# Mamba scan: softplus as one table function on ScalarE, and a seventh group per step with du by DMA

## The chip, the cores and the metric

The kernel runs on one core of a Trainium2 chip. The metric is the device time of one execution in microseconds. The core has five engines with an instruction queue each: TensorE (PE), VectorE (DVE), ScalarE (ACT), GpSimd (POOL) and SyncE (SP, which here only issues DMAs), and 16 DMA engines beside them.

## The reference

The reference is a chain of four blocks on an image of shape 4 x 96 x 64 x 64: Mamba, an SSD block, Mamba again (other weights), and a ConvNeXt block. The change touches the two Mamba blocks alone. A Mamba block has two layers, each over a sequence of 4096 tokens:

```python
dbl = xc @ xproj_w
dt = dbl[..., :DTRANK]
Bm = dbl[..., DTRANK:DTRANK + DSTATE]
Cm = dbl[..., DTRANK + DSTATE:]
delta = jax.nn.softplus(dt @ dt_w + dt_b)
A = -jnp.exp(A_log)
dA = jnp.exp(delta[..., None] * A)
dBx = delta[..., None] * Bm[:, :, None, :] * xc[..., None]
...
hstates = jax.lax.associative_scan(comb, (dA, dBx), axis=1)[1]
y = jnp.einsum('blds,bls->bld', hstates, Cm) + Dp * xc
y = y * jax.nn.silu(z)
return y @ out_w
```

Here 192 channels have 16 states each, so that a layer has 3072 independent first-order recurrences. `xc` is the convolved input after SiLU, `z` the gate.

## The kernel before

`program` (L1799) runs `mamba_fusion`, `ssd`, `mamba_fusion`, `convnext` one after the other. A Mamba block is cut into **steps**: one image (4), one layer (2) and one chunk of 1024 tokens (4) make a step, so there are 32 steps in a block and 64 in the kernel.

A step has two parts. The **front** (`mamba_front`, L158) makes what the scan needs: layer norm, the in-projection joined with the convolution (L207, copied from PSUM at L213, SiLU over all three tiles at L215), the gate z (L223), `dbl` (L238 to L242), then softplus for three tiles of 128 x 512 (`begin`, L254: a matmul `pt` and `softplus`, L333). `softplus` works on ScalarE with the one table set that holds exp and ln: Abs, Exp, Ln, and two Identity passes that recover the rounding lost in 1 + u. The rest of it is one VectorE operation per tile (`rest`, L266) and two GpSimd operations (`lost` L270, `size` L274). `sized` (L277) makes du = delta * x on GpSimd. delta and du go to DRAM (`store`, L282, as dd and dg), and B and C come back from DRAM copied over the partitions (L293, tile bc).

The **scan** (`Scan`, L346) cuts a step into 24 **groups** of 128 x 1024 (8 channels of each half of the tokens by 16 states): three tiles j, four quarters q, two halves p, in this order. I call a group's number in its step, 0 to 23, its place. For each group:

- `load` (L363) fetches delta rows from DRAM, copied over the 16 states (da, two DMAs of 256 KB);
- `spread` (L375): in an ordinary group TensorE spreads du into PSUM (bs, L384). In a **DMA group** du comes by two more DMAs from dg, ScalarE writes the exponential of da to bs in PSUM instead, and `product` (L390) multiplies du by B on GpSimd (L392);
- `decay` (L398): the exponential of da in place, on ScalarE, in an ordinary group;
- `scan` (L402) on VectorE: in an ordinary group first the product of bs and B (L407), then the recurrence along the tokens (L412);
- `after` (L415): GpSimd multiplies the states by C (hc, L419), ScalarE copies the last column (carry, L422);
- `sums` (L424), `close` (L445) and `project` (L452): TensorE adds over the states into py, VectorE multiplies by the gate (y, L450), TensorE projects.

Before the change a step has six DMA groups, at places 1, 5, 9, 13, 17 and 21. Which comes when is written out by hand in `run` (L472): iteration n calls the stages for groups at fixed distances (load 5 ahead, spread 1 ahead, decay and product 2 ahead, scan at n, after 1 behind), then advances the front of the next step by a number of its `yield` segments that the table PACE (L324) gives, then py's sums and the projections. What is recorded so is chained in order on each engine (L537 to L542): each engine runs its instructions strictly in this order. The front of the next step begins 8 groups before the step ahead of it starts (LEAD), so PACE's entry k falls in place (k + 16) mod 24. The front of the very first step of a block runs alone, ahead of the scan.

ScalarE's table sets are kept by `Tables` (L96): `exp_ln` uses the standing set; `other` loads another set first and, with `back`, the standing set again behind it.

Buffers that matter: tile tag da (da and du loads) has 8, bs in PSUM 2, the front's PSUM tag mm 2, hs 4, hc 5.

## Time and profile before

| What | Value |
|---|---|
| median of 3 runs | 8700.51 us (8700.26 to 8705.55) |
| the profiled execution's own time | 8698.77 us |
| its span | 8697.1 us |
| mean granted TensorE clock | 0.93 |
| busy over the span: PE, DVE, ACT, POOL | 84%, 88%, 66%, 79% |
| first Mamba scan, 76 to 2900 us: DVE, POOL, ACT busy | 2614, 2588, 1819 us of 2824 |
| SSD, 2900 to 5000 us: DVE, POOL, ACT busy | 1698, 1403, 1613 us of 2100 |
| second Mamba scan, 5400 to 8100 us: DVE, POOL, ACT busy | 2557, 2556, 1760 us of 2700 |
| DMA share in the same three stretches | 0.83, 0.33, 0.85 |

The profile is of one execution. Busy time of an engine is the time in which one of its instructions runs; the DMA share is the mean busy share of the 16 DMA engines. A group is all instructions of one line, engine, operation and shape, with its count, its busy time and the mean length of one; what follows is the engine's idle time just before them and who ended it. In a timeline each row has start, length, engine, line, operation and tiles, and in brackets the idle time ahead of it with the instruction that ended it. An instruction's length is longer than its distance to the next one where both overlap.

### The profile page before, as it was taken

To read this page: it belongs to the slowest core of one execution; us is meant where nothing else is said; L and a number is where in the kernel's file an instruction comes from. 1 tells how busy PE (TensorE), PEld (TensorE's weight loads), DVE (VectorE), ACT (ScalarE), POOL (GpSimd) and SP (SyncE) were. 2 spreads that over 40 slices of the span, in tenths; PEclk is the share of its full clock that TensorE was granted. 3 is DMA by queue.
4 is the path that set the end of the run, shared out by engine and by line. 5 is a ranking of instruction groups with operands and counts; after the bars stand their busy time and mean duration, and the time that the engine had idled before them with its cause. 6 is when DMAs were issued, how large, how long until landed. Compare 5 with 4: busy or idle time off the path is not lost. (4 is left out here: it accounts for less than half of the span.)

```text
span 8697.1 us, 112655 instructions
## 1 busy us (share of the span) xinstructions
PE 7340.2 (84%) x34200; PEld 3243.1 (37%) x34200; DVE 7621.2 (88%) x8769; ACT 5778.7 (66%) x10726; POOL 6909.6 (79%) x4653
## 2 busy tenths in 40 slices
PE   7888888888887898998988887888888888887588
PEld 1222222222221687887887884122222222221122
DVE  6999999999998687887888886999999999999786
ACT  5666667666664777777777776666666666666255
POOL 6999999999998565665766765999999999999321
PEclk8999999999998899999999998999999999999799
DMA  6888888888886323333333234888888888888553
GB/s 176 221 223 235 219 222 229 221 225 227 226 220 178 105 88 98 101 90 96 103 94 105 86 90 118 214 220 232 224 219 229 224 226 225 229 222 222 127 126 80
DMA packets 800712, 1524.98 MB, mean 175 GB/s; under 512 B 115565, under 2 KB 121481, under 8 KB 797034
## 3 DMA queue, kind: packets, MB, share of 16 engines
q1 hardware_dynamic: 797034, 1512.67, 65.8%
q8 instruction: 273, 4.47, 0.2%
q10 hardware_dynamic: 3072, 5.11, 0.2%
q14 instruction: 333, 2.73, 0.1%
HBM read 1222.55 MB, written 148.50 MB: 158 GB/s over the span
## 5 line engine op out<-in xcount | busy, mean ns | idle before, releaser
L419 POOL TENSOR_TENSOR hc<-hs,bc 128x1024 f32<-128x1024 f32 x1536 | 3602.1, 2360 | 299.9 <-DVE hs L412 291.6
L412 DVE TENSOR_TENSOR_SCAN hs<-da,carry,bs 128x1024 f32<-128x1024 f32 x864 | 2027.4, 2347 | 129.2 <-issue 51.7
L384 PE MATMUL bs<-du,seldu 64*128 64x512 f32 x4608 | 1481.1, 709 | 684.0 <-DVE hs L412 667.5
L407 DVE TENSOR_TENSOR bs<-bs,bc 128x1024 f32<-128x1024 f32 x1152 | 1396.9, 1213 | 20.3 <-PE bs L384 19.6
L110 ACT ACTIVATE da<-da,w_a 128x1024 f32<-128x1024 f32 x1152 | 1301.7, 1139 | 1.5
L384 PEld LDWEIGHTS bs<-du,seldu 64*128 64x128 f32 x4608 | 409.7, 202 | 1765.8 <-issue 894.9
L433 PE MATMUL py<-hc,selsum 128*32 128x512 f32 x6144 | 876.2, 633 | 92.3 <-DVE y L450 63.3
L392 POOL TENSOR_TENSOR du<-du,bc 128x1024 f32<-128x1024 f32 x384 | 907.5, 2363 | 12.3 <-DMA du<-dg 12.3
L110 ACT ACTIVATE bs<-da,w_a 128x1024 f32<-128x1024 f32 x384 | 428.5, 1116 | 583.9 <-DVE hs L412 459.5
L207 PE MATMUL pu<-h,w_conv 96*64 96x512 f32 (+1 forms) x3072 | 808.3, 645 | 7.8 <-ACT h L196 7.2
L1334 POOL TENSOR_TENSOR y<-y,xs 128x192 f32<-128x192 f32 x496 | 292.9, 591 | 654.5 <-DVE y L1327 615.6
L412 DVE TENSOR_TENSOR_SCAN hs<-bs,carry,du 128x1024 f32<-128x1024 f32 x288 | 670.7, 2329 | 58.6 <-DMA dd<-delta 34.3
L1155 DVE SCALAR_TENSOR_TENSOR bc<-front,taps,bc 128x342 f32<-128x342 f32 (+1 forms) x1152 | 656.9, 571 | 64.1 <-ACT bc L1147 35.9
L412 DVE TENSOR_TENSOR_SCAN hs<-da,bs 128x1024 f32<-128x1024 f32 x288 | 658.4, 2286 | 42.0 <-issue 15.1
L110 ACT ACTIVATE seg<-seg,ndac 128x128 f32<-128x128 f32 x1536 | 502.8, 390 | 246.8 <-POOL seg L1234 244.7
L1123 PE MATMUL front<-sconv,pk 128*128 128x192 f32 x3072 | 606.6, 335 | 0.4
L1265 POOL TENSOR_TENSOR xs<-x,coef 128x576 f32<-128x576 f32 x512 | 589.5, 1151 | 16.7 <-DVE y L1343 14.7
L1234 POOL TENSOR_TENSOR seg<-dr,mask 128x384 f32<-128x384 f32 x512 | 511.5, 999 | 8.3 <-DMA dr<-rows 8.3
L1123 PEld LDWEIGHTS front<-sconv,pk 128*128 128x128 f32 x3072 | 517.0, 196 | 2.7 <-ACT dtrow L900 1.3
L1680 DVE SCALAR_TENSOR_TENSOR acc<-strips,kern,acc 128x512 f32<-128x512 f32 x504 | 426.1, 847 | 53.2 <-ACT acc L1670 36.7
L463 PE MATMUL po<-y,w_out 64*96 64x512 f32 x768 | 446.2, 679 | 0.0
L422 ACT COPY carry<-hs 128x1 f32<-128x1 f32 x1152 | 203.4, 180 | 363.5 <-DVE hs L412 362.8
(231 smaller groups left out, 13504.6 us busy)
## 6 DMA issues: line engine op xcount, KB each, us to landing
da<-dd SPq DMA_DIRECT2D x3072, 256.0 KB
du<-dg SPq DMA_DIRECT2D x768, 256.0 KB
dr<-rows SPq DMA_DIRECT2D x256, 384.0 KB
bc<-rows SPq DMA_DIRECT2D x256, 256.0 KB
dd<-delta SPq DMA_DIRECT2D x192, 256.0 KB
dg<-du SPq DMA_DIRECT2D x192, 256.0 KB
pk<-xn SPq DMA_DIRECT2D x128, 384.0 KB
pk<-xn SPq DMA_DIRECT2D x128, 256.0 KB
```

Of the source, the lines that this page charges most:

```text
L110: self.last = self.scalar.activation(out, in_, func, **kw)
L207: nc.tensor.matmul(pu[HALFP * i : HALFP * (i + 1)], lhsT=wt["conv"][:kk, tap, D0[j] : D0[j] + HALFP], rhs=h[:kk, ds(i * T + tap, T)], star ...
L384: nc.tensor.matmul(g["bs"][:, i], lhsT=self.sel["du"][rows, g["half"], g["q"]], rhs=g["made"]["du"][rows, g["j"]], start=True, stop=True,)
L392: self.tc.nc.gpsimd.tensor_tensor(g["du"], g["du"], self.b_or_c(g, 0), ALU.mult)
L407: nc.vector.tensor_tensor(dbx, dbx, self.b_or_c(g, 0), ALU.mult)
L412: nc.vector.tensor_tensor_scan(out, da, dbx, init, ALU.mult, ALU.add)
L419: nc.gpsimd.tensor_tensor(g["hc"], hs, self.b_or_c(g, 1), ALU.mult)
L433: nc.tensor.matmul(py[ds(HALFP * i + QUART * x["half"], QUART)], lhsT=self.sel["sum"][:, q], rhs=x["hc"][:, i], start=(q == 0), stop=(q == ...
L1123: nc.tensor.matmul(p, lhsT=held["pk"][:, i, ds(c * Q, Q)], rhs=self.conv[:, i], start=(i == 0), stop=(i == 2),)
L1155: nc.vector.scalar_tensor_tensor(out, shifts[tap], self.taps[:, q, tap : tap + 1], out, ALU.mult, ALU.add)
L1234: self.nc.gpsimd.tensor_tensor(seg, g["pair"]["dr"][:, ds(g["c"] % 2 * NH, NH)], self.mask[:, g["r"]].to_broadcast([P, NH, Q]), ALU.add,)
L1265: self.nc.gpsimd.tensor_tensor(xs, x.to_broadcast([P, 3, NH, HD]), coef.to_broadcast([P, 3, NH, HD]), ALU.mult)
```

## The change

Softplus becomes one table function (Softplus) on ScalarE, for three tiles in a row between two loads of table sets. The VectorE operation and two of the three GpSimd operations per tile go, and with them tile v. Place 7 becomes a DMA group in each step, so there are seven: 1, 5, 7, 9, 13, 17 and 21. Tag da gets 9 buffers. PACE is written anew: with it SiLU of x moves from place 5 to place 7, all three softplus tiles fall in place 13 (before: 11, 12 and 14), bc's loads in 14 (before: 13). Tag ua has 3 buffers in all its uses, and the layer norm's rs has two of its own. An unused helper `softplus_tail` goes too.

```diff
-    kept = []
-    def begin(j):
-        pt = bank("pt")
...
-        kept.append(softplus(nc, k.act, work, pt))
-    def rest(j):
-        delta, t, u, v, x = kept[j]
-        nc.vector.scalar_tensor_tensor(delta, x, 0.0, t, ALU.max, ALU.add)
-    def lost(j):
-        u, v = kept[j][2:4]
-        nc.gpsimd.tensor_tensor(v, u, v, ALU.subtract)
-    def size(j):
-        delta, v = kept[j][0], kept[j][3]
-        nc.gpsimd.tensor_tensor(delta, delta, v, ALU.add)
+    def sizes():
+        deltas = []
+        for j in range(3):
+            pt = bank("pt")
+            for i in range(2):
+                half = ds(HALFP * i, HALFP)
+                nc.tensor.matmul(
+                    pt[half], lhsT=wt["dt"][half, D0[j] : D0[j] + HALFP], rhs=dbl[half], start=True,
+                    stop=True,
+                )
+            delta = work.tile([P, T], F32, name="delta", bufs=3)
+            k.act.other(delta, pt, AF.Softplus, back=(j == 2))
+            deltas.append(delta)
+        return deltas
     def sized(j):
-        nc.gpsimd.tensor_tensor(du[:, j], kept[j][0], made["x"][:, j], ALU.mult)
+        nc.gpsimd.tensor_tensor(du[:, j], deltas[j], x[:, j], ALU.mult)
...
-    begin(0)
+    deltas = sizes()
     yield
-    begin(1)
-    yield
-    rest(0)
-    lost(0)
     for i in range(2):
         for q in range(2):
...
+    sized(0)
     yield
-    size(0)
-    rest(1)
-    begin(2)
-    yield
-    sized(0)
-    lost(1)
-    rest(2)
+    store(0)
     gate(2)
     yield
-    store(0)
-    size(1)
-    yield
     sized(1)
-    lost(2)
     yield
     store(1)
-    size(2)
     yield
     sized(2)
...
 PACE = {
-    0: 2, 1: 1, 2: 1, 3: 1, 4: 1, 6: 1, 7: 2, 8: 2, 9: 1, 10: 1, 11: 2, 12: 2, 13: 1, 15: 1, 16: 2,
-    17: 1, 18: 1, 19: 1, 20: 1, 21: 1, 22: 1, 23: 1, 24: 1, 25: 1, 26: 1, 27: 1, 28: 1, 29: 1,
+    0: 2, 1: 1, 2: 1, 3: 1, 4: 1, 6: 1, 7: 1, 8: 2, 9: 1, 10: 1, 11: 1, 12: 2, 13: 1, 14: 1, 15: 1,
+    16: 1, 17: 2, 18: 1, 19: 1, 21: 1, 22: 1, 23: 1, 25: 1, 26: 1, 27: 1, 28: 1, 29: 1,
 }
...
-            g[name] = self.state.tile([P, GS, T], F32, tag="da", name=name, bufs=8)
+            g[name] = self.state.tile([P, GS, T], F32, tag="da", name=name, bufs=9)
...
-                last=(q == NQU - 1 and p == 1), dma=(q % 2 == 0 and p == 1),
+                last=(q == NQU - 1 and p == 1), dma=(p == 1 and (q % 2 == 0 or (j, q) == (0, 3))),
```

## The prediction

> **What bounds the kernel now.** I took the busy line by stage first, since the change touches only the two Mamba scans; then the groups of one such stage, then the engines' timelines over one step. The busy line is for 450 to 2450 us (columns: stretch, length, PE, PEld, DVE, ACT, POOL, granted clock, DMA share, GB/s):

> ```profile
> 450.00:2450.00 2000.00, 1707.96 (x6655) 417.39 (x6654) 1900.77 (x1191) 1339.67 (x2067) 1907.01 (x923) 0.94 0.86 225
> ```

> VectorE and GpSimd are both 95% busy; ScalarE has a third free. One step of 24 groups takes 84.67 us (the same y close, L450, stands at 1200.85 and 1285.52 in VectorE's timeline), and there are 64 steps (dd is stored 192 times, 3 a step). The groups of 600 to 2400 us, with count, busy time and mean:

> ```profile
> L419 POOL TENSOR_TENSOR hc<-hs,bc 128x1024 f32<-128x1024 f32 x512 | 1200.0, 2358 | 84.5 <-DVE hs L412 81.6 <-PE py L433 1.3 <-DMA da<-dd 1.2
> ...
> L407 DVE TENSOR_TENSOR bs<-bs,bc 128x1024 f32<-128x1024 f32 x383 | 464.5, 1213 | 2.6 <-PE bs L384 2.5
> ...
> L392 POOL TENSOR_TENSOR du<-du,bc 128x1024 f32<-128x1024 f32 x127 | 299.9, 2362 | 0.0
> ...
> L274 POOL TENSOR_TENSOR delta<-delta,v 128x512 f32<-128x512 f32 x63 | 80.4, 1276 | 0.0
> ...
> L266 DVE SCALAR_TENSOR_TENSOR delta<-pt,lg 128x512 f32<-128x512 f32 x63 | 41.9, 665 | 0.0
> ```

> GpSimd waits for VectorE's scans (hc), so VectorE leads most of the time. Its timeline shows where it doesn't, once a step, at the sixth DMA group (place 21):

> ```profile
> 1259.28 2.35 DVE L412 TENSOR_TENSOR_SCAN hs<-da,carry,bs 128x1024 f32<-128x1024 f32 x1
> 1262.92 2.35 DVE L412 TENSOR_TENSOR_SCAN hs<-bs,carry,du 128x1024 f32<-128x1024 f32 x1 [1.29 <-POOL du L392]
> ```
> ```profile
> 1256.98 1.28 POOL L274 TENSOR_TENSOR delta<-delta,v 128x512 f32<-128x512 f32 x1
> 1258.23 2.35 POOL L419 TENSOR_TENSOR hc<-hs,bc 128x1024 f32<-128x1024 f32 x1
> 1260.54 2.35 POOL L392 TENSOR_TENSOR du<-du,bc 128x1024 f32<-128x1024 f32 x1
> ```

> B's product ends at 1262.89, the scan starts at 1262.92: GpSimd was late, having the nine short softplus operations between its products. The stalls of this kind sum to 27.7 us in 1800, or 1.3 a step. (Most are put down to a DMA of dd, but there too the product ends last: at 1008.64 for a scan at 1008.68.) From one start to the next, as instructions overlap, a scan takes 2.26 us, a DMA group's 2.24, L407 1.36 with its hand-over, L266 0.58.

> Last, ScalarE's timeline around SiLU of x, which now falls in place 5:

> ```profile
> 1205.22 0.19 ACT L422 COPY carry<-hs 128x1 f32<-128x1 f32 x1 [0.93 <-DVE hs L412]
> 1207.52 0.58 ACT L213 COPY x<-pu 128x512 f32<-128x512 f32 x1 [2.11 <-PE pu L207]
> 1208.12 1.28 ACT L115 ACT_TABLE_LOAD   x1
> 1209.41 1.48 ACT L115 ACTIVATE x<-x 128x1536 f32<-128x1536 f32 x1
> 1210.91 1.28 ACT L122 ACT_TABLE_LOAD   x1
> 1212.21 1.15 ACT L110 ACTIVATE da<-da,w_a 128x1024 f32<-128x1024 f32 x1
> ```

> Scan 5 began at 1205.10; ScalarE is free for exponentials again 7.11 us later. The next one that VectorE needs straight from PSUM (bs of place 9) is three groups off, so this costs nothing today.

> [...] the trace has 0.58 to 0.69 for its ScalarE operations of 512. [...]

> **The change, part by part.** Durations are the profiled execution's (8698.77 us, span 8697.1; 1.7 below the median).

> *Softplus on VectorE and GpSimd.* Three L266 go: 3 x 0.58 = 1.74 us a step from the engine that bounds. Six short GpSimd operations go, 6 x 1.245 = 7.5 us, and with them the stall at place 21, 1.3 us: behind product 21 only one `sized` is left in that place, and the hc ahead of it is no longer late. What is late next is VectorE itself.

> *Seventh DMA group, place 7.* VectorE loses one L407 and gains 0.02 on the scan: 1.36 + 0.02 = 1.38 us. GpSimd gains one product, 2.33; its sum is 31 x 2.33 + 3 x 1.245 = 76.0 us a step, under VectorE's. Places 5, 7 and 9 are crowded: from the end of scan 4 GpSimd does hc 4, product 7, hc 5, hc 6, product 9, five times 2.33 = 11.7 us, and VectorE reaches scan 9 at 2.24 + 3.62 + 2.24 + 3.62 = 11.7: just in time, counted as nothing. PE loses two matmuls, nothing. SP issues two more DMAs, 1.2 us of a queue that waits 516 of these 1800 us for buffers; the ninth buffer lets it load as far ahead as before (30 tiles in 8, 31 in 9). DMA: a step's 0.86 x 84.67 = 72.8 us is some 72.5 transfers of 256 KB, 1.0 us each; two more make 74.8. In 600 to 2400 us I counted packets off against issues: a da load lands 2.2 to 7.4 us after issue, and its load is called five groups ahead, so nothing here.

> Gain: 1.74 + 1.30 + 1.38 = 4.42 us in a step with a front beside it.

> *Given back, place 9.* The new pace puts SiLU of x in place 7, and the compiled order of ScalarE has carry 6, the x copy, load, SiLU, load, and directly after it the exponential of bs 9. Zero is the start of scan 7: ScalarE is free at 7.11 (the chain above, the same PE work ahead of it), bs 9 is there at 7.11 + 1.12 + 0.05 = 8.28. VectorE has scan 7 (now a DMA group, no L407), L407 8 and scan 8: 2.24 + 1.36 + 2.26 = 5.86, and scan 9 has nothing else to do. **Stall 2.4 us.** Queued behind it is VectorE's whole row; GpSimd waits with it.

> *Given back, place 15.* The three softplus matmuls now stand together in place 13 (a DMA group, 2.24 us long), ahead of the projection and of bs 15. PE from the start of scan 13: hand-over 0.23, bs 14 1.06, three pt of 1.04, projection 1.03, bs 15 1.06: 6.5 us. VectorE wants bs 15 at 5.86. **Stall 0.7 us** with its hand-over. Softplus itself isn't in the trace: I take 0.6 us; below 0.58 no operation of that shape lies, above I bound it by SiLU's 1.48, three times as long. At 0.6 it ends the third at 5.1 and the exponential of place 16 at 7.5, needed at 9.5: hidden. ScalarE: load 1.28, three at 0.6, load 1.28 in place of 3 x 3.1 us. The third pt reuses the first one's PSUM bank (there are two): at 0.6 softplus 0 frees it at 3.0 and PE gets there at 3.4, at 1.48 PE waits and the stall grows by 0.6.

> *Other moves.* bc's four loads start one place later (14), needed by place 1 of the next step: nothing. First dd and dg are stored one place earlier, nothing. The two fronts ahead of the scans (at 40 to 76 us and near 5360) run uncovered: ScalarE spends 48.92 to 62.34 from the first Abs to the last load, some 8.5 with the table function, and first loads go out at 61.1 after GpSimd's chain; I take 5 us each, between 0 and 7.

> Sum for each scan of 32 steps: 32 x 1.38 + 31 x (1.74 + 1.30) - 31 x (2.4 + 0.7) = 44.2 + 94.2 - 96.1 = 42.3 (31, as the last step has no front beside it). Two scans and two starts: 84.6 + 10 = 95 us. **8700.5 - 95 = 8605**, a step of 83.3 us. Its own range: the stalls of 2.4 and 0.7 may be 0.4 off each way (62 x 0.8 = 50) or the softplus at 1.48 (37): 8555 to 8660.

> **Rivals.** *The two stalls don't come* (PE or ScalarE gets ahead in a way that I don't see): 44.2 + 94.2 doubled is 277, plus 10: 8414. For it: VectorE never waits long for ScalarE now. Against: the order on ScalarE is fixed, and its chain is measured.

> *DMA becomes the bound.* The place is the loads of da and du in every step, the price set by the busy share s that 16 engines can hold: a step is 74.8 / s. The share that I forecast is 74.8 / 83.3 = 0.90. From s under 0.90 it eats the gain, at 74.8 / 84.67 = 0.883 nothing is left, at today's 0.86 a step is 87.0, so 64 x 2.3 = 147 us slower: **8850**. For it: 0.86 is already the highest of any stage, and over bc's loads and the stores (1235 to 1255) it stands at 0.9 to 1.06. Against: that very stretch shows that 0.9 and more can be held, landings stay under 7.4 us, SP waits for buffers and not for transfers.

> **Chances.** Forecast 0.68; stalls absent 0.08; DMA mild (s of 0.883 to 0.90, so 8605 to 8700) 0.12, half of it within 0.2% of before; DMA in full 0.12, slower. Within 0.2%, some 17 us, is about what a measurement of this kernel can't tell from no change. Faster 0.68 + 0.08 + 0.06 = 0.82, same 0.06, slower 0.12. The range 8540 to 8700 leaves out the absent stalls and the DMA in full, 0.20.

> **What would show it.** Right: VectorE's timeline with one stall of about 2.4 us before the scan of place 9, named bs L110 or a table load, one of about 0.7 before L407 of place 15, none at place 21; GpSimd at about 92%; steps of 83.3 us; DMA share 0.90. Wrong: scans of places 1, 5 or 7 waiting for products whose du landed late (DMA); a softplus row over 1.5 us; or no wait at place 9.

## The result and the profile after

The changed kernel takes 8714.94 us (median of 20 runs, 8695.17 to 8723.24) against 8703.34 before (20 runs, 8698.19 to 8709.78), a ratio of 1.0013 with a 95% interval of 1.0006 to 1.0019: 12 us slower where 95 us faster was forecast. The profiled execution is one of the faster ones: 8705.49 us, with a span of 8703.7.

The busy line of the same stretch as before (450 to 2450 us; PE, PEld, DVE, ACT, POOL, granted clock, DMA share, GB/s):

```profile
450.00:2450.00 2000.00, 1663.53 (x6535) 404.86 (x6534) 1825.47 (x1091) 1229.31 (x1818) 1782.88 (x800) 0.94 0.89 230
```

VectorE went from 95 to 91%, GpSimd from 95 to 89%: the work was taken off as meant, and the time wasn't. The wait is in the groups of the whole page (count, busy and mean, then idle time ahead and who ended it), first of the kernel before, then of the changed one:

```profile
L407 DVE TENSOR_TENSOR bs<-bs,bc 128x1024 f32<-128x1024 f32 x1152 | 1396.9, 1213 | 20.3 <-PE bs L384 19.6
```
```profile
L360 DVE TENSOR_TENSOR bs<-bs,bc 128x1024 f32<-128x1024 f32 x1088 | 1319.1, 1212 | 131.6 <-PE bs L337 130.4
...
L365 DVE TENSOR_TENSOR_SCAN hs<-bs,carry,du 128x1024 f32<-128x1024 f32 x336 | 782.4, 2329 | 140.3 <-ACT bs L110 94.8
```

L360 is the old L407 and L365 the old L412; on TensorE, L337 is the old L384 (bs) and L196 the old L207 (the convolution taps). Before, L407 had waited 20 us in all for TensorE; now it is 130, and the DMA groups' scans wait for ScalarE's exponential into bs. One step of VectorE's timeline shows both, in places 7, 8, 8 and 9:

```profile
947.41 2.32 DVE L365 TENSOR_TENSOR_SCAN hs<-bs,carry,du 128x1024 f32<-128x1024 f32 x1
952.21 1.23 DVE L360 TENSOR_TENSOR bs<-bs,bc 128x1024 f32<-128x1024 f32 x1 [2.48 <-PE bs L337]
953.53 2.35 DVE L365 TENSOR_TENSOR_SCAN hs<-da,carry,bs 128x1024 f32<-128x1024 f32 x1
959.12 2.35 DVE L365 TENSOR_TENSOR_SCAN hs<-bs,carry,du 128x1024 f32<-128x1024 f32 x1 [3.24 <-ACT bs L110]
```

I numbered all scans of the trace by place and added up VectorE's waits of over 0.25 us ahead of each, for the middle 30 steps of each block, 60 in all. Per step, in us:

| kernel | step | place 8 | place 9 | place 15 | place 21 | all waits | step less waits |
|---|---|---|---|---|---|---|---|
| before | 85.07 | 0.03 | 0.00 | 0.02 | 1.39 | 1.74 | 83.33 |
| after | 85.26 | 1.27 | 3.06 | 0.44 | 0.00 | 5.02 | 80.24 |

The work of a step fell by 3.09 us and the waits grew by 3.28. The wait at place 9 is the forecast one, larger; its chain on ScalarE, in the step shown:

```profile
953.22 0.59 ACT L202 COPY x<-pu 128x512 f32<-128x512 f32 x1 [5.50 <-PE pu L196]
953.82 1.28 ACT L115 ACT_TABLE_LOAD   x1
955.12 1.49 ACT L115 ACTIVATE x<-x 128x1536 f32<-128x1536 f32 x1
956.62 1.28 ACT L122 ACT_TABLE_LOAD   x1
957.91 1.12 ACT L110 ACTIVATE bs<-da,w_a 128x1024 f32<-128x1024 f32 x1
```

The wait at place 8 was in no line of the forecast. It comes from TensorE, which in that step reads as follows:

```profile
941.70 2.08 PE L337 MATMUL bs<-du,seldu 64*128 64x512 f32 x4 [2.60 <-DVE hs L365]
943.71 3.68 PE L196 MATMUL pu<-h,w_conv 96*64 96x512 f32 x8
947.33 2.08 PE L394 MATMUL py<-x,w_dd 128*128 128x512 f32 x2
949.33 1.77 PE L386 MATMUL py<-hc,selsum 128*32 128x512 f32 x8
951.03 1.13 PE L337 MATMUL bs<-du,seldu 64*128 64x512 f32 x4
```

The same four records of bs take 2.08 us at 941.70 and 1.13 at 951.03. The stretches around it (columns as above) say why:

```profile
937.19:940.60 3.41, 1.53 (x12) 0.19 (x8) 3.22 (x4) 2.75 (x4) 3.41 (x2) 1.00 0.50 153
```
```profile
940.60:950.80 10.20, 9.10 (x22) 2.01 (x22) 9.02 (x5) 2.65 (x5) 9.31 (x5) 0.50 0.96 243
950.80:957.70 6.90, 6.90 (x34) 1.61 (x32) 3.58 (x2) 4.43 (x4) 6.46 (x4) 1.00 0.48 110
```

TensorE was busy 1.53 of 3.41 us, and for the next 10.2 us its granted clock is 0.50. The bs at 951.03 is that of place 8, bs 8 for short. What stands ahead of it takes about twice as long, VectorE waits 2.5 us for it, and the tap and the SiLU chain behind it start late as well. In the kernel before, one tap alone, x's last, stands between the idle stretch and the bs of the next places:

```profile
1205.33 1.13 PE L384 MATMUL bs<-du,seldu 64*128 64x512 f32 x4 [2.20 <-DVE hs L412]
1206.39 1.08 PE L207 MATMUL pu<-h,w_conv 97*64 97x512 f32 x4
1207.48 1.13 PE L384 MATMUL bs<-du,seldu 64*128 64x512 f32 x4
```

**Theories.** Mine, after seeing this: two causes. *Order*: the new pace puts SiLU's two table loads right ahead of the exponential of bs 9. *Clock*: after a stretch in which it is little busy (1.53 of 3.41 us here), TensorE runs at half clock (0.50 for 10.2 us), and the new pace leaves more convolution taps behind that stretch: two stand between it and bs 8 (943.71, eight records) and a third, the one that SiLU needs, right behind bs 8. Rivals: *transfers* (da and du land late at the higher DMA share), and *overfull TensorE* (too much work ahead of bs 8 at any clock).

### The profile page after: what moved, and what is told of

Its sections match the earlier page's. It is cut to its first block, busy times and chain, and to the rows that moved or that the text cites. A ratio compares the mean times of both kernels' runs of the same rounds, so it can differ in the third digit from the quotient of the medians.

```text
span 8703.7 us, 110981 instructions
## 1 busy us (share of the span) xinstructions
PE 7265.9 (83%) x33944; PEld 3230.3 (37%) x33944; DVE 7427.8 (85%) x8513; ACT 5500.8 (63%) x10086; POOL 6599.4 (76%) x4333
## 5 line engine op out<-in xcount | busy, mean ns | idle before, releaser
L372 POOL TENSOR_TENSOR hc<-hs,bc 128x1024 f32<-128x1024 f32 x1536 | 3606.3, 2358 | 604.6 <-DVE hs L365 513.7
L337 PE MATMUL bs<-du,seldu 64*128 64x512 f32 x4352 | 1387.1, 687 | 785.0 <-DVE hs L365 765.6
L365 DVE TENSOR_TENSOR_SCAN hs<-da,carry,bs 128x1024 f32<-128x1024 f32 x816 | 1914.6, 2346 | 119.0 <-issue 50.8
L360 DVE TENSOR_TENSOR bs<-bs,bc 128x1024 f32<-128x1024 f32 x1088 | 1319.1, 1212 | 131.6 <-PE bs L337 130.4
L110 ACT ACTIVATE da<-da,w_a 128x1024 f32<-128x1024 f32 x1088 | 1231.3, 1139 | 4.3 <-DMA da<-dd 2.8
L110 ACT ACTIVATE bs<-da,w_a 128x1024 f32<-128x1024 f32 x448 | 501.0, 1118 | 912.7 <-DVE hs L365 606.3
L345 POOL TENSOR_TENSOR du<-du,bc 128x1024 f32<-128x1024 f32 x448 | 1057.8, 2361 | 25.4 <-DMA du<-dg 13.1
L337 PEld LDWEIGHTS bs<-du,seldu 64*128 64x128 f32 x4352 | 391.3, 198 | 1769.8 <-issue 967.6
L365 DVE TENSOR_TENSOR_SCAN hs<-bs,carry,du 128x1024 f32<-128x1024 f32 x336 | 782.4, 2329 | 140.3 <-ACT bs L110 94.8
L196 PE MATMUL pu<-h,w_conv 96*64 96x512 f32 (+1 forms) x3072 | 845.9, 665 | 9.0 <-ACT h L185 7.2
L110 ACT ACTIVATE seg<-seg,ndac 128x128 f32<-128x128 f32 x1536 | 502.9, 390 | 248.9 <-POOL seg L1187 246.5
L365 DVE TENSOR_TENSOR_SCAN hs<-da,bs 128x1024 f32<-128x1024 f32 x272 | 621.9, 2286 | 38.9 <-issue 15.9
L1272 PEld LDWEIGHTS y<-xs,seg 128*128 128x128 f32 x3072 | 426.3, 197 | 26.8 <-DVE seg L1208 0.5
```

The lines of the kernel that those rows point to most:

```text
L110: self.last = self.scalar.activation(out, in_, func, **kw)
L196: nc.tensor.matmul(pu[HALFP * i : HALFP * (i + 1)], lhsT=wt["conv"][:kk, tap, D0[j] : D0[j] + HALFP], rhs=h[:kk, ds(i * T + tap, T)], star ...
L337: nc.tensor.matmul(g["bs"][:, i], lhsT=self.sel["du"][rows, g["half"], g["q"]], rhs=g["made"]["du"][rows, g["j"]], start=True, stop=True,)
L345: self.tc.nc.gpsimd.tensor_tensor(g["du"], g["du"], self.b_or_c(g, 0), ALU.mult)
L360: nc.vector.tensor_tensor(dbx, dbx, self.b_or_c(g, 0), ALU.mult)
L365: nc.vector.tensor_tensor_scan(out, da, dbx, init, ALU.mult, ALU.add)
```

## The experiments

Each was timed beside runs of the kernel before on the same chip (medians 8702.76 to 8704.78 us); ratios are to those. "Half clock" is the share of the time between two scans' starts that falls in stretches of clock 0.50.

### Six DMA groups again

```diff
-dma=(p == 1 and (q % 2 == 0 or (j, q) == (0, 3))),
+dma=(q % 2 == 0 and p == 1),
```

> The changed kernel with only the six old DMA groups; the rest stays. Clock and order (my theory: TensorE's granted clock falls to half where place 7 leaves it idle, and SiLU's block of table loads stands right ahead of the exponential of bs 9): place 7 is an ordinary group again, which costs 1.4 us a step; TensorE keeps its clock, the 1.3 us before L360 of place 8 go, the wait before scan 9 falls from 3.1 to about 1.0 as scan 9 is wanted 1.4 us later. Net 1.95 us a step less: about 8595 us. Transfers (rival: da and du land late at a DMA share of 0.89): all of the stalls go, about 8535. Overfull TensorE (rival: there is too much work ahead of bs 8 at any clock): the wait at place 8 stays, about 8675.

Measured: 8699.98 us, 0.9997 (0.9989 to 1.0006). All three expectations missed. Place 7 is ordinary again and the wait at place 8 falls to 0.18 us a step, but that before scan 9 only to 2.36, as TensorE still stands at half clock in 43% of place 5 and 31% of place 6. In the 25 of 60 steps where it doesn't, scan 9 waits 1.43 (not the expected 1.0; perhaps since bs 7 now stands ahead of bs 8 on TensorE, which no run tests), in the others 3.02. So with the new pace TensorE slows down without the seventh group too. The group has a part in it all the same: with it the half clock of places 5, 6 and 7 is 53, 72 and 39% of the time, without it 43, 31 and 4%, and scan 8 is wanted one L360 sooner.

### Keeping TensorE busy at place 7

TensorE spreads du into bs of place 7 too; the exponential then overwrites it.

```diff
         for i in range(GS):
+            if g["dma"] and (g["j"], g["q"]) != (0, 3):
+                break
             rows = ds(HALFP * i, HALFP)
...
+        if g["dma"]:
+            self.exps(g, g["bs"])
```

> The changed kernel, with place 7 still a DMA group, but TensorE spreads du into bs of place 7 as well, to be overwritten by the exponential: two matmuls more, of no use to the result. Clock and order: TensorE keeps its clock, the 1.3 us before place 8 go and the wait before scan 9 falls from 3.1 to 2.4: 1.9 us a step, about 8595 us. Transfers: nothing changes, 8715. Overfull TensorE: the two matmuls make bs 8 later by up to 1.1 us a step, 8715 to 8780.

Measured: 8724.14 us, 1.0016 (1.0006 to 1.0026). It missed what clock and order had, and came nearest to "overfull"; it decides nothing between clock and "overfull", as places 5 and 6 stay slow. The clock gets better only behind the added matmuls (half clock 53, 42 and 0% in places 5, 6 and 7, against 53, 72 and 39), place 8's wait falls to 0.36, but the exponential of bs 7 now waits for the matmuls (0.63 at place 7) and scan 9 still waits 3.14. The edit comes too late to keep the clock, and it adds a wait.

### SiLU of x in place 6

```diff
-0: 2, 1: 1, 2: 1, 3: 1, 4: 1, 6: 1, 7: 1, 8: 2, 9: 1, 10: 1, 11: 1, 12: 2, 13: 1, 14: 1, 15: 1,
+0: 2, 1: 1, 2: 1, 3: 1, 4: 1, 6: 1, 7: 1, 8: 2, 9: 1, 10: 1, 11: 2, 12: 2, 13: 1, 14: 1,
```

> The changed kernel with PACE entries 11 and 15 altered, so that x's last tap and SiLU fall in place 6, behind the exponential of bs 7 and three groups ahead of scan 9, not in place 7. Clock and order: the wait before scan 9, 3.1 us a step, goes (190 us); the one at place 8 stays at 1.3 or grows to 2, as one more convolution tap stands ahead of bs 8 at half clock: 8530 to 8600 us. Transfers: 8715. Overfull TensorE: the wait at place 8 grows by 2 us or so in each step, about 8650.

Measured: 8515.46 us, 0.9782 (0.9766 to 0.9798), 200 us below the changed kernel, by one segment of the front taken from entry 15 and put into entry 11, which brings the last taps and SiLU one place forward. VectorE's timeline of one step, places 7 to 9:

```profile
1575.74 2.33 DVE L365 TENSOR_TENSOR_SCAN hs<-bs,carry,du 128x1024 f32<-128x1024 f32 x1
1579.57 1.23 DVE L360 TENSOR_TENSOR bs<-bs,bc 128x1024 f32<-128x1024 f32 x1 [1.50 <-PE bs L337]
1580.89 2.35 DVE L365 TENSOR_TENSOR_SCAN hs<-da,carry,bs 128x1024 f32<-128x1024 f32 x1
1583.15 2.32 DVE L365 TENSOR_TENSOR_SCAN hs<-bs,carry,du 128x1024 f32<-128x1024 f32 x1
```

Scan 9 waits no more (0.04 a step), place 8 still does (0.66), place 15 more than before (1.18). Order is shown; transfers are out, as DMA now has a share of 0.92 and no wait of note is for it. It beat the lower end of what was expected, as place 8's wait shrank instead of growing: two taps stand ahead of bs 8 as before the edit, not one more, and half clock in places 5, 6 and 7 fell to 27, 45 and 26%. A tap more now lies ahead of the idle stretch, which may be why.

### SiLU in place 6 and the matmuls of place 7

Both edits above.

> Both edits together: SiLU of x in place 6, and the two useless matmuls of place 7 that keep TensorE busy. Clock and order: the waits at places 8 and 9 both go, 4.3 us a step: about 8450 us, a step of 81 us. Transfers: 8715, or more as the scans ask for data faster. Overfull TensorE: 8650 or more.

Measured: 8515.27 us, 0.9783 (0.9769 to 0.9798): no different. Place 8 falls to 0.32, place 7 gets 0.14, place 15 stays at 1.18. My 8450 was wrong: the matmuls of place 7 leave 0.46 at places 7 and 8, and place 15, which I had left out, waits 1.18 where the changed kernel has 0.44.

### A tap of place 4 three times

The first tap of x's third tile lies in place 4, before TensorE's idle stretch. It is issued three times, each a full overwrite.

```diff
+            copies = 3 if (j, tap) == (2, 0) else 1
+            for m in range(copies):
                 for i in range(2):
                     nc.tensor.matmul(
...
-                    rhs=h[:kk, ds(i * T + tap, T)], start=(tap == 0), stop=(tap == 3),
+                        rhs=h[:kk, ds(i * T + tap, T)], start=(tap == 0),
+                        stop=(tap == 3 or m < copies - 1),
```

> The changed kernel; the first convolution tap of x's third tile, which falls in place 4, is issued three times instead of once (the last time counts, the result is the same). It lies in TensorE's idle time ahead of bs 6 and waits for nothing new. Clock: in the changed kernel places 5 to 7 run at half TensorE clock in 53, 72 and 39% of their time, after a stretch in which TensorE was under some 0.6 busy; with the stretch filled the clock holds, the wait at place 8 falls from 1.3 to 0.3 us a step and the one before scan 9 from 3.1 to 2.5: about 8620 us. Overfull TensorE (rival: it has too much work there whatever its clock): the 2.1 us more of work make places 8 and 9 wait as long or longer, 8715 to 8800.

Measured: 8607.22 us, 0.9888 (0.9873 to 0.9903). Useless work on an engine made the kernel 108 us faster. Half clock in places 5 to 7 is 2, 3 and 1%; place 8 has no wait left. VectorE's timeline, places 7 to 9 (this kernel's L363 and L368 are L360 and L365 above):

```profile
1021.92 2.33 DVE L368 TENSOR_TENSOR_SCAN hs<-bs,carry,du 128x1024 f32<-128x1024 f32 x1
1024.16 1.21 DVE L363 TENSOR_TENSOR bs<-bs,bc 128x1024 f32<-128x1024 f32 x1
1025.46 2.35 DVE L368 TENSOR_TENSOR_SCAN hs<-da,carry,bs 128x1024 f32<-128x1024 f32 x1
1030.24 2.35 DVE L368 TENSOR_TENSOR_SCAN hs<-bs,carry,du 128x1024 f32<-128x1024 f32 x1 [2.43 <-ACT bs L110]
```

Scan 9 waits 2.43 in this step and 2.49 on average: the forecast 2.4, with the clock held. Overfull TensorE falls, clock is shown. Not all is gain: place 15 now waits 0.96 and not 0.44, as half clock in place 13 rises from 12 to 35%.

### SiLU in place 6, repeats in places 4 and 11

To SiLU in place 6 and the tap of place 4 three times it adds the gate's second pair of matmuls three times, in place 11.

```diff
-        for i in range(2):
+        for i in [0, 1] * (3 if j == 1 else 1):
             nc.tensor.matmul(
                 pz[HALFP * i : HALFP * (i + 1)],
```

> SiLU of x in place 6, the tap of place 4 three times, and the gate's second matmul pair of place 11 three times too (all repeated work, same result), each in idle time of TensorE. Clock: the waits left with SiLU in place 6, 0.6 us at place 8 and 1.15 at place 15, fall to about 0.1 and 0.7, the latter being the one of full clock: about 8455 us. Overfull TensorE: 8515 or more.

Measured: 8439.88 us, 0.9696 (0.9682 to 0.9711), the fastest of all and faster than both kernels. The step is 81.0 us with 0.6 of waits. VectorE's waits from 600 to 2400 us, first of the changed kernel, then of this one (total, times, longest):

```profile
DVE hs L365 <- ACT bs L110: 58.9, 45, 3.3
...
DVE bs L360 <- PE bs L337: 42.4, 37, 2.7
```
```profile
DVE bs L363 <- PE bs L340: 12.1, 33, 1.8
...
DVE hs L368 <- ACT bs L110: 5.0, 21, 0.5
```

Place 15 waits 0.14 us a step, not the 0.7 that I had for full clock.

### Softplus alone

Six DMA groups, and the pace of before up to its entry 18, with SiLU of x in place 5.

```diff
...
+0: 2, 1: 1, 2: 1, 3: 1, 4: 1, 6: 1, 7: 2, 8: 2, 9: 1, 10: 1, 11: 2, 12: 2, 13: 1, 15: 1, 16: 2,
+17: 1, 18: 1, 21: 1, 22: 1, 23: 1, 25: 1, 26: 1, 27: 1, 28: 1, 29: 1,
...
```

> The softplus half of the change alone: one table function, three tiles in a row in place 13, with six DMA groups and the old pace up to place 10, so that SiLU of x stays in place 5 as before the change. By my sum: 3.0 us a step less (1.7 on VectorE, 1.3 of the stall at place 21), 0.7 to 1.2 back at place 15: about 8575 us, between 8550 and 8600. Rival (the loads of table sets around softplus are what costs): no faster than 8690.

Measured: 8535.06 us, 0.9810 (0.9793 to 0.9826). Half of the change alone gives 170 us, somewhat more than expected, in part since place 15 waits 0.60 and not 0.7 to 1.2. The two more table loads a step (1.28 us each in the changed kernel's trace) cost nothing that shows.

### Six groups, SiLU in place 6

> Six DMA groups, table softplus, SiLU of x in place 6: the run with SiLU in place 6 less the seventh group. By my sum the seventh group is worth 1.4 us a step when no wait answers to it, and place 8's 0.6 us go without it: 0.8 us net, so about 8565 us against 8515. Transfers (rival: at a DMA share of 0.92 the seventh group's loads hold the scans up): 8515 or less.

Measured: 8583.53 us, 0.9859 (0.9845 to 0.9874). The seventh group is worth 68 us here (8515.46 with it), where 50 were expected; transfers are out again. Place 8 waits 0.81 and place 11 0.40, with half clock in places 5, 6 and 9 (34, 39, 44%): the wait of place 8 doesn't need the seventh group either.

### SiLU in place 6, repeats in place 4 only

> SiLU of x in place 6 and the tap of place 4 three times, without the repeats of place 11. Order and clock, as two causes that add up: against SiLU in place 6 alone (8515) the 0.6 us at place 8 go, about 8477 us; place 15 keeps its 1.15 us a step. If the repeats at place 4 were worth the 108 us that they brought to the changed kernel, 8407.

Measured: 8508.31 us, 0.9777 (0.9763 to 0.9792), 7 below SiLU in place 6 alone and not 38. Place 8's 0.66 go as expected; place 15 goes from 1.18 to 1.48, as half clock in place 13 rises from 51 to 67%. With the repeats of place 11 that share was under 10% and the wait 0.14: the gain of one place was handed to the next slow stretch.

### Eight buffers for da and du

```diff
-self.state.tile([P, GS, T], F32, tag="da", name=name, bufs=9)
+self.state.tile([P, GS, T], F32, tag="da", name=name, bufs=8)
```

In the fastest kernel.

> SiLU of x in place 6 with both repeats (8440), and 8 buffers for da and du in place of 9. My theory: loads land within some 8 us and are called five groups ahead, and the ninth buffer is worth little: 8440 to 8470 us. Transfers (rival: DMA at a share of 0.93 stands just short of the bound): loads start a group later and the scans wait for products, 8550 or more.

Measured: 8444.44 us, 0.9703 (0.9689 to 0.9718): 5 us more than with nine, hardly to be told apart. With eight buffers too the loads come in time, at a DMA share of 0.94 here.

### The seventh group at place 3

```diff
-dma=(p == 1 and (q % 2 == 0 or (j, q) == (0, 3))),
+dma=(p == 1 and (q % 2 == 0 or (j, q) == (0, 1))),
```

with the pace of softplus alone.

> Seven DMA groups with the seventh at place 3 (j 0, q 1) in place of 7, the pace of the run with softplus alone, so SiLU of x in place 5 with no exponential of a DMA group behind it before place 9. Order: none of the two waits of places 8 and 9 is there and the seventh group's 1.4 us a step come in full, 8535 - 88, about 8447 us. Clock: TensorE gets idle around place 3 and reaches its taps at half clock, so up to 1.4 us a step comes back: 8535. The seventh group as such is the fault (rival): 8650 or more.

Measured: 8515.46 us, 0.9784 (0.9768 to 0.9800), on the side of the clock, though in another place than I had said. Places 8 and 9 don't wait. Place 15 waits 1.83 in every one of the 60 steps, with half clock in 99% and more of places 12 and 13:

```profile
944.70 1.23 DVE L359 TENSOR_TENSOR bs<-bs,bc 128x1024 f32<-128x1024 f32 x1 [1.83 <-PE bs L336]
```

Seven groups are no fault in themselves: this kernel has seven and is 187 us faster than the one before.

### The repeats in the kernel before

> The kernel before the change, with the first tap of x's third tile three times (place 3 there). A control: places 5 and 6 stand at half clock in 45 and 39% of their time, but VectorE doesn't wait for TensorE there. Clock costs only where TensorE is late: same as before, within 15 us of 8704. If repeats of matmuls made any kernel faster: 8600.

Measured: 8699.82 us, 0.9997 (0.9989 to 1.0006). Half clock goes from places 5 and 6 (45 and 39%, now none) and nothing is won. In this kernel a slow TensorE costs nothing there, as VectorE isn't waiting for it.

## Why the prediction was wrong

**Softplus off VectorE and GpSimd, 1.74 + 1.30 us a step: right.** The wait at place 21 is gone (1.39 to 0.00), and the work of a step fell by 3.09 us, where 1.74 and the seventh group's 1.38 make 3.12.

**Softplus at 0.6 us: right.** The group's row has 598 ns:

```profile
L115 ACT ACTIVATE delta<-pt 128x512 f32<-128x512 f32 x63 | 37.6, 598 | 46.4 <-PE pt L247 46.4
```

**DMA, SP and buffers at nothing: right.** The share is 0.89 in the changed kernel (0.90 forecast for a shorter step) and 0.93 in the fastest one. A da load lands 2.2 to 7.7 us after issue, median 3.6, as before (2.2 to 7.4, 3.6).

**GpSimd crowded around places 5 to 9, nothing: right.** No wait for a product in these places outlasts 0.25 us. In all of the 60 steps scan 9 starts 0.09 us after its exponential's end, and the product for it has been done for 2.1 us or more.

**Place 9, 2.4 us: the mechanism right, the size too small.** It is 3.06 in the changed kernel and 2.49 in the run that holds TensorE's clock. The difference lies in "the same PE work ahead of it": in the step shown TensorE reaches bs 8 3 us late, and then scan 9 waits 3.24, since L360 and the scan of place 8 take 3.6 from bs 8's end and the chain of tap, copy, load, SiLU, load and exponential 6.9.

**"PE loses two matmuls, nothing": this step failed.** I counted TensorE's work and not its clock. Place 8 waits 1.27 us where I had none, and place 9 gets some 0.6 more. The changed kernel's own trace shows it at one and the same order of work: in the 15 of its 60 steps with no half clock in places 5 to 7, place 8 doesn't wait in any and scan 9 waits 2.46; in the other 45 it is 1.69 and 3.25. The run with the tap repeated (more work for TensorE, 108 us faster) shows that holding the clock takes these waits away. The two matmuls aren't the whole of it: with six groups, 8700 us, TensorE is slowed all the same and the wait before scan 9 stays at 2.36. The new pace alone leaves two taps between the idle stretch and bs 8; the seventh group adds to the slow clock and wants scan 8 sooner. How much of place 8's wait is the group's, and how much the pace's, these runs don't part.

**Place 15, 0.7 us: near in size by chance, wrong in kind.** It is 0.44 on average in the changed kernel: 1.82 in the 12 of 60 steps with half clock in places 12 to 14, 0.09 in the others. TensorE's timeline in a step at full clock:

```profile
973.09 1.13 PE L337 MATMUL bs<-du,seldu 64*128 64x512 f32 x4 [1.58 <-DVE hs L365]
974.15 2.85 PE L247 MATMUL pt<-dbl,w_dt 64*64 64x512 f32 x12
976.93 0.67 PE L416 MATMUL po<-y,w_out 64*96 64x512 f32 x1
976.94 0.69 PE L337 MATMUL bs<-du,seldu 64*128 64x512 f32 x1
```

From start to start, the three pt take 2.78 us and not 3.12, and the projection and bs 15, which begin 0.01 us apart, take 1.88 us to the start of what follows (978.81) and not 2.09. That is 0.55 of the 0.7. What remains is half clock in place 13, and the wait follows its share over the runs: 0.14 at 3% (both places repeated), 0.96 at 35% (place 4 repeated), 1.18 at 51% (SiLU in place 6), 1.83 at 99% (the seventh group at place 3).

**The starts, 10 us: right in sum by chance.** The first scan begins at 67.6 us instead of 76.9, 9.3 earlier; the second block's begins 2586.1 us after the last scan of the first block began, instead of 2586.6, which is 0.5. The forecast had 5 each, and at most 7.

In sum 4.42 us a step were forecast to go and 4.48 went (3.09 + 1.39). 3.1 were forecast to come back at places 9 and 15, and 4.77 came at 8, 9 and 15: 1.67 us for 62 steps, 104 us, is the miss between 8605 and 8715 to within 6 us, and that to the profiled execution (8705.49) to within 4. Of the rivals neither happened: both waits came, and DMA didn't bind.

Not settled: why a given step meets the slow stretch and another doesn't. An explanation that no run tests is that a step (85.26 us, 24.98 times 3.413) isn't a multiple of that grid. The waits of places 8 and 15 come in part of the steps (41 and 26 of 60), and after repeats in place 4 alone there was more half clock in place 13.

## What to carry to other kernels

In a schedule written out by hand, look at what stands *behind* a moved instruction in its queue: here SiLU one place later cost 200 us, as it put a chain of 6.9 us, with SiLU and two table loads in it, in front of a scan that VectorE could have begun after 3.6. An engine with time to spare may still set the pace: TensorE was busy 83% of 450 to 2450 us in the changed kernel, at half clock in 53, 72 and 39% of places 5 to 7, and VectorE waited 1.27 us a step for it at place 8. Read the granted clock by stretches of a few us, at the places where others wait for it, not as a mean. And take the work removed and the waits apart in the trace before judging a change: this one took off the work that it was meant to, and half of it alone was 170 us faster than the kernel before.

## What the runs showed of the hardware

- TensorE's clock by how busy it was: cut on the 3.413 us grid on which the clock changed, the changed kernel's trace has, from 100 to 2800 us and at full clock, 76 stretches with TensorE under 50% busy, and in 63 cases the next one runs at half clock; of 123 at 50 to 70%, 13; of 477 above, none. In the kernel before it is 46 of 49, 32 of 110 and 1 of 515. Of the changed kernel's 63 + 13 stretches ahead of half clock, TensorE was busy for 20 to 50% in 61 and under 60% in 72. (How busy TensorE is rests on modelled ends of its matmuls.)
- Repeating a matmul pair in such a stretch (2.1 us of TensorE a step) made the kernel 108 us faster where it was waited for (8714.94 to 8607.22) and changed nothing where it wasn't (0.9997).
- Two matmul records on 64 rows each, of the projection and of bs, started 0.01 us apart (976.93, 976.94) and took 0.67 and 0.69 us; the two last of that bs, one after the other, took 0.59 each. Both tiles together took 1.88 us from start to start, where apart they take 1.03 and 1.06.
- Softplus took 598 ns for 128x512 from PSUM, about what ScalarE's copies of that shape took (576 and 582), and a table load 1.283 us; from 600 to 2400 us the next operation began 0.01 us behind it in 105 of 126 cases, and in the other 21 up to 2.77 us behind.
